# A graph attention layer on one core: the first group's projection goes behind the node table, and a ninth gather slot opens earlier

## The chip, the cores and the metric

The kernel runs on one core of a Trainium2 chip. The metric is the device time of one execution in microseconds (us); lower is better. A core has five engines with their own instruction queues: TensorE (PE in the profile, with its weight loads as PEld), VectorE (DVE), ScalarE (ACT), GpSimd (POOL) and SyncE (SP), which here only issues DMA transfers. Sixteen DMA engines carry all transfers of the core, whichever queue issues them.

## The reference

The input is a graph of 12500 nodes with 128 features each and 212500 edges, sorted by their target node, each with 128 features of its own. The layer computes, per edge, eight attention scores (one for each head of 16 features), and sums the messages at the target:

```python
Q = (x @ WQ).reshape(N, H, dh)
K = (x @ WK).reshape(N, H, dh)
V = (x @ WV).reshape(N, H, dh)
Eh = (edge_attr @ WE).reshape(-1, H, dh)
score = K[src] * Q[dst] / jnp.sqrt(jnp.float32(dh)) * Eh
score = jnp.exp(jnp.clip(score.sum(-1, keepdims=True), -5.0, 5.0))
msg = V[src] * score
wV = jax.ops.segment_sum(msg, dst, num_segments=N)
Z = jax.ops.segment_sum(score, dst, num_segments=N)
h = x + (wV / (Z + ATTN_EPS)).reshape(N, D)
# batch norm of h over the nodes, then layernorm(x + that) per node
```

The costly part is `K[src]` and `V[src]`: a row of 1 KB, from a place that the data chooses, for each of 212500 edges.

## The kernel before

**Tiling.** The edges are cut into 1661 tiles of 128, and the tiles into 208 groups of eight (the last has five). A group is two windows of four tiles; a window's edges point to at most some 64 successive nodes. The work for group g is a chain over the engines: `ehqe` projects the edge features (L560), copies them to `wt` on ACT (L562) and spreads the queries to the edges (L568); `both_halves` multiplies the two on VectorE (L573); `turn_back` transposes the product on PE (L581); `products` multiplies by the keys (L592); `scores` and `clip_exp` make the weights (L598, L606 to L608); `message` weights the values (L616); `onehot` (L521) and `gather_sum` sum the messages by node on PE (L631); `share`, or its steps `denom`, `recip` and `attn`, divides, and `add_x` and `x_out` add the result to `hx`, the transposed features. `q_window`, `q_mm` (L541), `q_hi`, `q_mid` and `q_lo` make a window's queries as three bf16 parts. `turned_onehot` (L531) makes the selection for L568 from target ids that `load_rel` fetches (L401); `load` fetches the edge features (L490).

**The node table.** Before the loop over groups, `table_rows(4 * q)` for q = 0 to 24 computes keys and values of 512 nodes at a time: PE multiplies (L676) into the PSUM banks `ps_e` and `ps_q`, `evac` copies them to a table buffer on ACT and VectorE in turn (L306, L307, L681), and SP stores the buffer to the table `kvd` in memory (L684, the last rows L687). The table buffers are tiles `t` of the pool `tab`, four in rotation, 4 KB per partition each.

**Gathers.** GpSimd gathers rows with one indirect DMA per tile (L225). The first eight groups do not wait for the table: 64 gathers fetch rows of x, and the kernel projects them itself. Groups 0 to 2 are projected among the table's blocks, and groups 3 to 7 in loops 2 to 6 by `project_main` (transposes L322, matmuls L329) into two table buffers each. From group 8 on, the rows come from `kvd` into one of the gather slots (`slot`, 8 KB per partition); these gathers wait for the whole table. In every eighth group or so, from group 18 on, the last tile comes row by row from SP instead (L277).

**Slots.** Eight slots, 0 to 7, exist from the start; four of them first hold the gathered rows of x for groups 0 to 7. `load_kv` takes a free slot and the next pending group and queues its gathers. A slot becomes free when `message(g)` has read it, or when `project_main` has turned the last rows of x in it. Slot 8 is made later: at the end of loop 7 (`FIRST_ROW - 1`) the pool `tab` is closed, a pool `late` is opened in its place, and slot 8, the row buffers `byrow` and the id buffers `rbq` are made in `late`. So group 16 comes into slot 8 and group 17 into the slot that group 8 leaves.

**Order.** The order of each engine's instructions is the order of the program text (`manual_schedule`); semaphores come from the data. In a loop g, `issue()` hands the queued gathers to GpSimd. From g = 8 (`FIRST_ROW`) on, `pace(step)` first makes one of them wait for that loop's `q_mm` on PE as well; whatever is behind it on GpSimd waits with it.

**Early steps.** `steps` lists work for the first groups that is put between the table's blocks, from q = 8 on, one entry per block. Its last entries are `ehqe(0)` and `both_halves(0)` at q = 21, `turn_back(0)`, `q_mm(2)` and `q_hi(2)` at q = 22 and `q_mid(2)` at q = 23. Behind the table come `load_kv()`, `ehqe(1)`, `onehot(0)`, `load(2)`, `turned_onehot(2)`, `load_rel(3)`, `q_window(3)`, `load_rel(4)`, `load(3)`, and then loop 0.

**The end.** When no group is pending, `load_x` puts pieces of x for the last stage into free slots (L477). Slot 8 is left out of that, since its pool closes before the last stage.

Of the kernel before, what the change touches and what calls it, by code (L numbers as in the profile page):

```python
# [8 lines left out]
F32 = mybir.dt.float32  # L9
# [8 lines left out]
P = 128  # L18
# [3 lines left out]
G = 8  # L22
# [3 lines left out]
NSLOT = 8  # L26
# [4 lines left out]
FIRST_ROW = 8  # L31
# [8 lines left out]
def plan(N, T):  # L40

    n, r = divmod(T - sum(LAST), U)
    sizes = [U] * n + [r] * (r > 0) + list(LAST)
    assert n > 1 and len(sizes) % 2 == 0
    starts = [sum(sizes[:g]) for g in range(len(sizes))]
    cuts = list(range(0, N - 64, CH)) + [N - 64, N]
    due = {}
    thr = [0.0] * len(sizes)
    for j, c in enumerate(cuts[1:]):
        need = (c + (64 if c < N - CH else 24)) * T  # L50
        g = next((g for g, t in enumerate(starts) if t * N >= need), None)
        if g is not None:
            due.setdefault(g, []).append(j)
            thr[g] = float(c)
    return sizes, starts, cuts, due, thr
# [27 lines left out]
def gnn_kernel(  # L83
# [23 lines left out]
    usizes, ustarts, cuts, due, _ = plan(N, T)  # L107
# [9 lines left out]
    rows = ctx.enter_context(tc.tile_pool(name="rows", bufs=1))  # L117
# [5 lines left out]
    tab = tps.enter_context(tc.tile_pool(name="table", bufs=1))  # L123
    late = []
# [85 lines left out]
    free = list(range(NSLOT))  # L210
    pending = list(range(nxg, NG))
# [1 line left out]
    steady = [False]  # L213

    def slot(i):
        return (rows if i < NSLOT else late[0]).tile([P, 2 * G * P], F32, name=f"slot{i}")

    def kv_view(g, t):
        SLOT[g] = t[0]
# [9 lines left out]
    queued = []  # L229
# [18 lines left out]
    for (_, n), groups in zip(ROW_STREAMS, row_plan(usizes)):  # L248
# [6 lines left out]
        if tot % n:  # L255
            q = tot // n
# [22 lines left out]
    def load_kv():  # L279
        while free and pending and table[0]:  # L280
            g = pending.pop(0)
            i = free.pop(0)
            kv_view(g, (i, slot(i)))
            for j in range(sizes[g] - (g in by_row)):
                queued.append((gather, KV[g](j, j + 1, 0, 2 * P).rearrange("p a d -> p (a d)"), kvd,
                               starts[g] + j))
            if not steady[0]:
                issue()

    for g in range(nxg):  # L290
        if g % 2 == 0:
            PAIR[g // 2] = free.pop(0)
            t = slot(PAIR[g // 2])
# [198 lines left out]

    def project_main(g):

        half = [tab.tile([P, 4, 2 * P], F32, name="t", bufs=4) for _ in range(2)]
        KV[g] = lambda a, b, c, n=P: half[a // 4][:, a % 4:a % 4 + b - a, c:c + n]
        turn_x(g, 0, True)
        turn_x(g, 4, True)
        yield
        for a in (0, 4):  # L500
            project(g, a, lambda: turned().rearrange("p (a b) d -> p a (b d)", b=2), True)
            yield
# [36 lines left out]
    def q_mm(g):  # L539
        PQ[g] = small_ps[:, 0, :]  # L540
        return nc.tensor.matmul(PQ[g], XW[g], w_q, start=True, stop=True)  # L541

    def q_hi(g):
        Q3[g] = wp.tile([P, 3, P], BF16, name="q3", bufs=2)
        nc.scalar.activation(Q3[g][:, 0, :], PQ[g], AF.Copy, scale=0.25)

    def q_mid(g):
        QR[g] = wp.tile([P, P], F32, name="qr", bufs=1)
        nc.vector.scalar_tensor_tensor(QR[g], PQ[g], 0.25, Q3[g][:, 0, :], op0=OP.mult, op1=OP.subtract)
        nc.scalar.activation(Q3[g][:, 1, :], QR[g], AF.Copy)  # L550
# [4 lines left out]
    def ehqe(g):  # L555

        QE[g], WT[g] = [], []
        for a, b in halves(g):
            eh = psp.tile([P, U * P], F32, name="ps_e", bufs=2)[:, :(b - a) * P]
            nc.tensor.matmul(eh, w_e, EA[g][:, a:b, :].rearrange("p a b -> p (a b)"), start=True, stop=True)  # L560
            t = wp.tile([P, U * P], F32, name="wt", bufs=2)
            nc.scalar.activation(t[:, :(b - a) * P], eh, AF.Copy)  # L562
            WT[g].append(t)
            QE[g].append(psp.tile([P, U * P], F32, name="ps_q", bufs=2)[:, :(b - a) * P])
        for k in range(3):
            for h, (a, b) in enumerate(halves(g)):
                r = slice(h * WN, (h + 1) * WN)
                nc.tensor.matmul(QE[g][h], Q3[g][r, k, :], OT[g][r, :(b - a) * P], start=(k == 0), stop=(k == 2))  # L568
# [6 lines left out]
    def turn_back(g):  # L575

        PW[g] = []
        for h, (a, b) in enumerate(halves(g)):
            ps = turned()
            for j in range(b - a):  # L580
                nc.tensor.transpose(ps[:, j, :], WT[g][h][:, j * P:(j + 1) * P], ident)  # L581
            PW[g].append(ps)
# [84 lines left out]
    NB = -(-N // P)  # L667

    def table_rows(b):
        t = tab.tile([P, 4, 2 * P], F32, name="t", bufs=4)  # L670
        for q in range(b, min(b + 4, NB), 2):
            ps = wide()
            m = min(2, NB - q)
            for i in range(m):
                n = min(P, N - (q + i) * P)
                nc.tensor.matmul(ps[:n, i, :], hx[:, (q + i) * P:(q + i) * P + n], w_kv, start=True, stop=True)  # L676
            fl = min(m, N // P - q)
            if fl:
                step = evac(t[:, q - b:q - b + fl, :], ps[:, :fl, :])
            if fl < m:  # L680
                nc.vector.tensor_copy(t[:n, q - b + fl, :], ps[:n, fl, :])  # L681
        full = min(4, N // P - b)
        if full > 0:
            nc.sync.dma_start(kvd[b * P:(b + full) * P, :].rearrange("(c p) d -> p c d", p=P), t[:, :full, :])  # L684
        if b + 4 > N // P and N % P:
            r0 = N // P * P
            nc.sync.dma_start(kvd[r0:N, :], t[:N - r0, N // P - b, :])  # L687
        while len(queued) > max(0, nxg * G - 11 - 12 * (b // 4 + 1) // 5):
            pace(step)

    NQ = -(-NB // 4)
# [4 lines left out]
    def both_halves(g):  # L696
        both(g, 0)
        both(g, 1)


    steps = [[(locate,)], [(place, runs[0])], [], [(q_mm, 0), (q_hi, 0)],
             [(q_mid, 0), (load_rel, 0)], [(q_lo, 0), (load, 0)], [(q_mm, 1), (q_hi, 1), (load_rel, 1)],
             [(q_mid, 1)], [(q_lo, 1), (load_rel, 2)], [(load, 1)], [(turned_onehot, 0)],
             [(turned_onehot, 1)], [], [(ehqe, 0), (both_halves, 0)], [(turn_back, 0), (q_mm, 2), (q_hi, 2)],
             [(q_mid, 2)]]
    first_step = NQ - len(steps) - 1
    assert first_step > 3 and max(piece) < first_step + 14
    windows = {first_step + 2: (0, 1), first_step + 8: (2,)}
    for q in range(NQ):
# [5 lines left out]
        for g, a in piece.get(q, []):  # L715
            if a == 0:
                i = free.pop(0)
# [11 lines left out]
        f(*a)  # L729
    table[0] = True  # L730
    load_kv()
    ehqe(1)
    onehot(0)
    within(load, 2)
# [48 lines left out]
    for g in range(NG - 2):  # L783
        within(load, g + 4)
        within(load_rel, g + 5)
        if (g + 6) % RQ == 0 and (g + 6) // RQ in quads:
            load_quad((g + 6) // RQ)
        fetch_rows(g)
        within(products, g)
        within(both_halves, g + 1)  # L790
        step = within(add_x, g - 3)
        step = within(q_mm, g + 3) or step
        if step is not None and queued and g >= FIRST_ROW:
            pace(step)
        issue()
        within(gather_sum, g - 1)
        if g + 1 < nxg and g + 1 not in SLOT:
            for _ in project_main(g + 1):
                pass
        within(turn_back, g + 1)  # L800
        within(scores, g)
        within(clip_exp, g)
        within(q_hi, g + 3)
        within(x_out, g - 3)
        within(sums_out, g - 1)
        within(q_lo, g + 2)
        within(denom, g - 2)
        within(recip, g - 2)
        within(attn, g - 2)
        within(q_window, g + 4)  # L810
        within(turned_onehot, g + 3)
        within(ehqe, g + 2)
        within(q_mid, g + 3)
        within(message, g)
        within(onehot, g + 1)
        if g == 2:
            load_last()
        for r in runs[1:]:
            if g == max(4, r[0] // 2 - 12):
                place(r)  # L820
        within_checks(g)
        if NSLOT in free and not pending:
            free.remove(NSLOT)
        while free and todo and not pending:
            load_x()
        bn_parts(2 * g - 5, 2 * g - 3)
        if g == NG - 5:
            assert done >= set(range(NPRE))
            norm_first()
        if g == 4:  # L830
            nc.vector.tensor_scalar(row_ids, row_ids, 8 * P, None, op0=OP.mult)
        if g == FIRST_ROW - 1:
            tps.close()
            late.append(tps.enter_context(tc.tile_pool(name="late", bufs=1)))
            free.append(NSLOT)
            load_kv()
    last = NG - 1
    g = last - 1
# [10 lines left out]
    step = add_x(g - 3)  # L849
# [315 lines left out]
```

## Time and profile before

| what | us |
|---|---|
| median of 3 runs | 2115.63 |
| fastest and slowest of them | 2113.8 and 2118.93 |
| the profiled execution | 2117.82 |
| its span, first to last instruction | 2116.0 |
| mean granted clock of TensorE | 0.928 |

A page of the profile gives busy time by engine, the costliest groups of instructions and the chain that ended last. A row of a group reads: line, engine, operation, what it writes and reads, how many, then its busy time and the mean of one in ns, and behind the second bar the time that the engine stood idle just before these instructions, and what ended most of that. A row of the timeline reads: start in us from the span's start, length in us, engine, line, operation, tiles, shapes, how many were merged into the row; in square brackets stands the idle time of the engine before it and what ended it. Rows of waits read: who waited on whom, total us, times, the longest. Where the releaser is called "issue", the engine waited for nothing that the profile shows. Windows by stretch give each engine's busy time and its number of instructions, then the granted clock of TensorE as a share of full speed, the busy share of the DMA engines and GB/s. Times inside the kernel are us from the start of the span.

### The profile page before, as it was taken

How to read it: one execution, taken by the hardware profiler on the slowest of the kernel's cores; microseconds unless marked ns; L12 is line 12 of the kernel's file. 1: busy time of each engine (PE TensorE's matmuls, PEld its weight loads, DVE VectorE, ACT ScalarE, POOL GpSimd, SP SyncE). 2: the span in 40 equal slices, each digit the busy share in tenths (PEclk: the TensorE clock that was granted, in tenths of full speed). 3: DMA queues.
4: the chain of work that ended last, by engine and by line, in shares of the span. 5: the costliest groups of instructions: out<-in, count | busy, mean ns of one | idle time of the engine just before them, and what ended most of it. 6: DMA issues, size and time to landing. Idle time of an engine off the chain costs nothing. (4 is left out here: it accounts for less than half of the span.)

```text
span 2116.0 us, 37688 instructions
## 1 busy us (share of the span) xinstructions
PE 1694.3 (80%) x9414; PEld 1103.1 (52%) x9414; DVE 1633.9 (77%) x3601; ACT 635.2 (30%) x2480; POOL 1581.2 (75%) x1673
## 2 busy tenths in 40 slices
PE   8899888887777777787877787878787788787877
PEld 6565555555454445455554554455455455454557
DVE  3559989997787787787777777777777778778777
ACT  2343333332232232222222232322222223223225
POOL 7776777777777777777777777777777777777775
PEclk9999999999999998999999999988999998999989
DMA  8856656666566555566565566565566555564674
GB/s 295 289 184 177 187 175 191 188 190 193 158 187 186 167 175 169 157 187 188 167 180 162 159 186 188 168 178 163 165 186 181 176 172 161 168 189 144 184 264 128
DMA packets 177913, 386.83 MB, mean 183 GB/s; under 512 B 38862, under 2 KB 94711, under 8 KB 177687
## 3 DMA queue, kind: packets, MB, share of 16 engines
q0 software_dynamic: 77552, 210.48, 33.9%
q1 hardware_dynamic: 95972, 171.08, 26.5%
q10 hardware_dynamic: 4163, 2.79, 0.4%
q8 instruction: 77, 1.26, 0.2%
q14 instruction: 149, 1.22, 0.2%
HBM read 364.58 MB, written 19.63 MB: 182 GB/s over the span
## 5 line engine op out<-in xcount | busy, mean ns | idle before, releaser
L225 POOL DMA_INDIRECT slot<-kvd,srcs x1573 | 1492.4, 949 | 487.5 <-issue 414.5
L631 PE MATMUL ps_a<-msg,oh 128*128 128x136 f32 (+1 forms) x3322 | 553.1, 308 | 1.7 <-DVE msg L616 1.7
L592 DVE TENSOR_TENSOR p<-slot,ps_t 128x512 f32<-128x512 f32 (+1 forms) x406 | 267.9, 673 | 323.6 <-DMA slot<-kvd,srcs 250.1
L631 PEld LDWEIGHTS ps_a<-msg,oh 128*128 128x128 f32 (+1 forms) x3322 | 447.6, 177 | 86.3 <-issue 61.7
L560 PE MATMUL ps_e<-ea,w_e 128*128 128x512 f32 x832 | 438.8, 654 | 27.7 <-DMA ea<-eaT 26.0
L607 ACT ACTIVATE ps_m<-s 128x64 f32<-128x64 f32 (+1 forms) x209 | 47.5, 227 | 1243.7 <-DVE s L606 931.4
L581 PE MATMUL ps_t<-ident,wt 128*128 128x128 f32 x1661 | 251.2, 293 | 118.0 <-DVE wt L573 116.4
L656 PE MATMUL ps_m<-ident,at 128*128 128x128 f32 x412 | 97.7, 320 | 227.8 <-DVE oh L524 222.9
L581 PEld LDWEIGHTS ps_t<-ident,wt 128*128 128x128 f32 x1661 | 196.3, 148 | 150.5 <-DVE wt L573 143.1
L573 DVE TENSOR_TENSOR wt<-wt,ps_q 128x512 f32<-128x512 f32 x416 | 265.6, 680 | 8.4 <-PE ps_q L568 7.2
L562 ACT ACTIVATE wt<-ps_e 128x512 f32<-128x512 f32 x416 | 233.5, 586 | 65.7 <-PE ps_e L560 61.8
L598 DVE TENSOR_REDUCE s<-p 128x64 f32<-128x1024 f32 (+1 forms) x209 | 251.9, 1205 | 0.1
L616 DVE TENSOR_TENSOR msg<-slot,ps_m 128x1024 f32<-128x1024 f32 (+1 forms) x205 | 242.2, 1182 | 1.4 <-ACT ps_m L607 1.0
L560 PEld LDWEIGHTS ps_e<-ea,w_e 128*128 128x128 f32 x832 | 158.9, 212 | 149.3 <-issue 110.7
L656 PEld LDWEIGHTS ps_m<-ident,at 128*128 128x128 f32 x412 | 63.6, 194 | 319.7 <-ACT q L550 297.1
L568 PE MATMUL ps_q<-ot,q 64*128 64x512 bf16 x1248 | 174.0, 385 | 0.0
L568 PEld LDWEIGHTS <-q 64*128 64x128 bf16 x1248 | 44.5, 95 | 196.7 <-issue 172.6
L521 DVE TENSOR_TENSOR oh<-ps_m,rel_i 128x512 f32<-128x512 f32 x208 | 142.0, 683 | 0.0
L510 ACT ACTIVATE xw<-hx 128x64 f32 x416 | 83.9, 248 | 66.4 <-issue 53.2
L661 ACT ACTIVATE hx<-ps_m 128x64 f32 x412 | 90.4, 219 | 8.0 <-PE ps_m L657 1.2
L647 DVE SCALAR_TENSOR_TENSOR at<-os,keep,rz 128x128 f32<-128x128 f32 x208 | 73.2, 352 | 25.1 <-PE ps_m L656 1.5
L541 PE MATMUL ps_m<-w_q,xw 128*128 128x128 f32 x416 | 86.2, 291 | 1.0 <-ACT xw L510 0.9
(172 smaller groups left out, 1553.7 us busy)
## 6 DMA issues: line engine op xcount, KB each, us to landing
ea<-eaT SPq DMA_DIRECT2D x207, 512.0 KB
byrow<-kvd SPq DMA_DIRECT2D x3072, 1.0 KB
slot<-kvd,srcs POOLq DMA_INDIRECT x1573
rbq<-relT SPq DMA_DIRECT2D x94, 256.0 KB
kvd<-t SPq DMA_DIRECT2D x24, 512.0 KB
slot<-xT SPq DMA_DIRECT2D x24, 256.0 KB
out<-o SPq DMA_DIRECT2D x23, 256.0 KB
hx<-xT SPq DMA_DIRECT2D x11, 512.0 KB
```

What stands on the lines that cost most here:

```text
L225: return nc.gpsimd.indirect_dma_start(out=out, out_offset=None, in_=table, in_offset=bass.IndirectOffsetOnAxis(ap=srcs[:, e:e + 1], axis=0))
L521: nc.vector.tensor_tensor(one, iota_ps[:, None, :].to_broadcast([P, n, P]), r[:, :n, None].to_broadcast([P, n, P]), op=OP.is_equal)
L560: nc.tensor.matmul(eh, w_e, EA[g][:, a:b, :].rearrange("p a b -> p (a b)"), start=True, stop=True)
L562: nc.scalar.activation(t[:, :(b - a) * P], eh, AF.Copy)
L568: nc.tensor.matmul(QE[g][h], Q3[g][r, k, :], OT[g][r, :(b - a) * P], start=(k == 0), stop=(k == 2))
L573: nc.vector.tensor_tensor(t, t, QE[g][h], op=OP.mult)
L581: nc.tensor.transpose(ps[:, j, :], WT[g][h][:, j * P:(j + 1) * P], ident)
L592: nc.vector.tensor_tensor(PR[g][:, c:d, :], KV[g](c, d, 0), PW[g][i][:, c - a:d - a, :], op=OP.mult)
L598: nc.vector.tensor_reduce(SS[g][:, a:b, :], PR[g][:, a:b, :].rearrange("p t (h d) -> p t h d", d=DH), axis=AX.X, op=OP.add)
L616: nc.vector.tensor_tensor(MSG[g][:, a:b, :P].rearrange("p t (h d) -> p t h d", d=DH), KV[g](a, b, P).rearrange("p t (h d) -> p t h d", d=D ...
L631: nc.tensor.matmul(AGG[g][WN if j >= n else 0:], OH[g][j], MSG[g][:, j, :], start=(j == 0), stop=(j == n - 1))
L656: nc.tensor.matmul(ps, AT[g], ident, start=True, stop=False)
```

## The change

Four things are done.

1. `ehqe(0)`, `both_halves(0)`, `turn_back(0)`, `q_mm(2)`, `q_hi(2)` and `q_mid(2)` leave `steps` and stand behind the table's last rows and `load_kv()`. `first_step` stays 8, so the other steps keep their blocks.
2. Slot 8 is made at the start, in the pool of the other slots. Its two halves serve as two of the four table buffers (`table_tile(q)` for q % 4 of 0 and 1); the pool `tab` keeps two. In `project_main`, even groups use the halves of slot 8 and odd groups the two buffers of `tab`, so group 6 is the last in slot 8.
3. Slot 8 is put on the list of free slots at the end of loop 6 instead of loop 7, and it may serve for pieces of x at the end.
4. `pace` begins with loop 12 instead of loop 8.

```diff
     def slot(i):
-        return (rows if i < NSLOT else late[0]).tile([P, 2 * G * P], F32, name=f"slot{i}")
+        return rows.tile([P, 2 * G * P], F32, name=f"slot{i}")
+
+    first = slot(NSLOT).rearrange("p (h c d) -> p h c d", h=2, d=2 * P)
+
+    def table_tile(q):
+        return first[:, q % 4] if q % 4 < 2 else tab.tile([P, 4, 2 * P], F32, name="t", bufs=2)
...
-        half = [tab.tile([P, 4, 2 * P], F32, name="t", bufs=4) for _ in range(2)]
+        half = [table_tile(2 * (g % 2) + a) for a in (0, 1)]
...
-        t = tab.tile([P, 4, 2 * P], F32, name="t", bufs=4)
+        t = table_tile(b // 4)
...
-             [(turned_onehot, 1)], [], [(ehqe, 0), (both_halves, 0)], [(turn_back, 0), (q_mm, 2), (q_hi, 2)],
-             [(q_mid, 2)]]
-    first_step = NQ - len(steps) - 1
+             [(turned_onehot, 1)]]
+    first_step = NQ - len(steps) - 5
...
     table[0] = True
     load_kv()
+    ehqe(0)
+    q_mm(2)
+    q_hi(2)
+    both_halves(0)
+    q_mid(2)
+    turn_back(0)
     ehqe(1)
...
-        if step is not None and queued and g >= FIRST_ROW:
+        if step is not None and queued and g >= FIRST_ROW + 4:
             pace(step)
...
-        if NSLOT in free and not pending:
-            free.remove(NSLOT)
         while free and todo and not pending:
             load_x()
...
         if g == FIRST_ROW - 1:
             tps.close()
             late.append(tps.enter_context(tc.tile_pool(name="late", bufs=1)))
+        if g == FIRST_ROW - 2:
             free.append(NSLOT)
             load_kv()
```

## The prediction

> **What bounds the kernel now.** I read the page's shares first, then the tile `slot` on GpSimd, then the waits, then the timeline of GpSimd, and only then the place of the change. On the page no engine is full:
>
> ```profile
> span 2116.0 us, 37688 instructions
> PE 1694.3 (80%) x9414; PEld 1103.1 (52%) x9414; DVE 1633.9 (77%) x3601; ACT 635.2 (30%) x2480; POOL 1581.2 (75%) x1673
> ```
>
> The instructions on `slot`, and the waits of GpSimd (total, times, longest), say otherwise:
>
> ```profile
> L225 POOL DMA_INDIRECT slot<-x,srcs x64: 940/944/1152, 3.2 to 82.3; - x64
> L225 POOL DMA_INDIRECT slot<-kvd,srcs x1573: 940/946/1276, 86.6 to 2062.2; - x197
> ...
> POOL slot L225 <- issue: 431.9, 1407, 3.4
> ...
> POOL slot L225 <- PE ps_m L541: 15.4, 34, 5.3
> ```
>
> 1573 gathers of the node table run from 86.6 to 2063.1: 1976.5 us. Each holds GpSimd 0.946 us and the next follows 0.30 later, so they come about every 1.25 us. The "idle" of 414 us is that 0.30 again and again. Only two waits are longer, 3.36 (under issue) and 5.34, and the timeline shows them:
>
> ```profile
> 82.31 0.94 POOL L225 DMA_INDIRECT slot<-x,srcs  x1 [0.30 <-DVE t L681]
> 86.61 0.94 POOL L225 DMA_INDIRECT slot<-kvd,srcs  x1 [3.36 <-issue]
> ...
> 156.57 0.95 POOL L225 DMA_INDIRECT slot<-kvd,srcs  x1 [0.30 <-issue]
> ...
> 165.33 0.95 POOL L225 DMA_INDIRECT slot<-kvd,srcs  x1 [0.30 <-issue]
> 171.62 0.94 POOL L225 DMA_INDIRECT slot<-kvd,srcs  x1 [5.34 <-PE ps_m L541]
> ...
> 181.62 0.95 POOL L225 DMA_INDIRECT slot<-kvd,srcs  x1 [0.30 <-PE ps_a L631]
> ```
>
> So the gathers are one unbroken stream with two holes, one where the table ends and one after group 15 (64 gathers from 86.61). The other engines follow the stream at the end: in the waits VectorE stands 250 us for gathers, and the chain that ended last begins with one.
>
> ```profile
> DVE p L592 <- DMA slot<-kvd,srcs: 250.1, 108, 6.6
> 2055.94 2.74 DMA slot<-kvd,srcs
> ```
>
> What shifts the stream shifts the end by as much. The tail from the last gather (2062.2) to 2116.0, 53.8 us, keeps its length. At most the two holes can go: 3.36 - 0.30 + 5.34 - 0.30 = 8.1 us.
>
> **The change: the table's end.** PE, VectorE and SP there:
>
> ```profile
> 72.61 1.88 PE L560 MATMUL ps_e<-ea,w_e 128*128 128x512 f32 x4
> 74.42 0.82 PE L568 MATMUL ps_q<-ot,q 64*128 64x512 bf16 x6
> 75.17 1.13 PE L676 MATMUL ps_e<-w_kv,hx 128*128 128x256 f32 x4
> ...
> 77.06 1.04 PE L581 MATMUL ps_t<-ident,wt 128*128 128x128 f32 x8
> 77.93 0.39 PE L541 MATMUL ps_m<-w_q,xw 128*128 128x128 f32 x2
> 78.15 1.03 PE L676 MATMUL ps_e<-w_kv,hx 128*128 128x256 f32 x4
> 80.75 1.02 PE L560 MATMUL ps_e<-ea,w_e 128*128 128x512 f32 x2
> 81.62 0.42 DVE L681 COPY t<-ps_e 84x256 f32<-84x256 f32 x1 [0.65 <-ACT t L306]
> 82.20 0.69 SPq L687 DMA_DIRECT2D kvd<-t  x1
> ```
>
> PE has no idle time in these rows, so it sets the pace. The moved PE steps are `ehqe(0)` (72.61 to 75.17, 2.56 us) and `turn_back(0)` with `q_mm(2)` (77.06 to 78.15, 1.09). Without them the table's last matmuls end 3.65 earlier, at 77.1, and the last store (L687) goes out at 78.55. Now that store is free 4.1 us after its issue (82.20 to 86.61 - 0.30). Then it is free at 82.65, before the x gathers' turn ends at 82.31 + 0.94 + 0.30 = 83.55. So the table's gathers start at 83.55, 3.06 earlier, with 0.9 us to spare. Beside PE the moved steps take ACT (two copies to `wt`, `q_hi(2)`, half of `q_mid(2)`) and VectorE (two multiplies, the other half of `q_mid(2)`); they issue no DMA. On SP the stores of the last rows and the loads behind them move up.
>
> **The first loops.** The moved work now lies between the table and loop 0:
>
> ```profile
> 82.94 0.38 SPq L490 DMA_DIRECT2D ea<-eaT  x1
> 83.37 2.37 SPq L401 DMA_DIRECT2D rb<-relT  x4
> 84.60 1.28 DVE L573 TENSOR_TENSOR wt<-wt,ps_q 128x512 f32<-128x512 f32 x2
> 89.01 3.78 PE L560 MATMUL ps_e<-ea,w_e 128*128 128x512 f32 x4 [2.42 <-DMA ea<-eaT]
> 89.81 0.36 DVE L531 TENSOR_SCALAR ot<-rb,wiota 128x512 bf16<-128x512 bf16 x1 [2.37 <-DMA rb<-relT]
> 90.28 1.21 DVE L616 TENSOR_TENSOR msg<-slot,ps_m 128x1024 f32<-128x1024 f32 x1
> 94.29 1.29 DVE L573 TENSOR_TENSOR wt<-wt,ps_q 128x512 f32<-128x512 f32 x2 [0.42 <-PE ps_q L568]
> ```
>
> After: PE runs `ehqe(0)` from 77.1 to about 79.85 (its second half waits until L681 empties the bank). VectorE multiplies both halves to 81.1, PE turns them back by 81.75 (it idles some 0.7 in between), then does `ehqe(1)` in 2.7 until 84.45. `both_halves(1)` on VectorE, 84.60 before, then starts near 84.55: the 3.65 us are spent on a chain that nothing covers now, and no more. But the loads of group 2's edges (L490) and group 3's ids (L401) are issued about 3.65 earlier, at 79.3 and 79.7. By their present 6.1 and 6.4 us (to 89.01 and 89.81) they land near 85.4 and 86.1. PE asked for them at 89.01 - 2.42 = 86.6 and VectorE at 89.81 - 2.37 = 87.4, and with `both_halves(1)` unmoved they still do. The waits of 2.37 and 0.42 on VectorE's line go. With about 0.2 lost behind ACT's `q_hi(3)` (my estimate from VectorE's line, which then has no slack there), the main loop runs 2.6 us earlier. I call that shift d = -2.6.
>
> [...] The rows by stretch, whose granted clock (PEclk) is the third number from the end, show it low just behind the 2.42 us wait:
>
> ```profile
> 86.00:90.00 4.00, 1.58 (x5) 0.85 (x6) 1.59 (x4) 0.97 (x5) 2.78 (x3) 0.70 0.97 260
> 90.00:96.00 6.00, 6.00 (x24) 2.71 (x23) 5.55 (x11) 1.39 (x3) 4.48 (x6) 0.63 0.98 334
> ```
>
> [...]
>
> **The second hole.**
>
> ```profile
> 153.45 1.04 PE L322 MATMUL ps_t<-ident,slot 128*128 128x128 f32 x8
> 160.25 1.27 DVE L616 TENSOR_TENSOR msg<-t,ps_m 128x512 f32<-128x512 f32 x2
> 170.96 0.39 PE L541 MATMUL ps_m<-w_q,xw 128*128 128x128 f32 x2
> 175.40 1.21 DVE L616 TENSOR_TENSOR msg<-slot,ps_m 128x1024 f32<-128x1024 f32 x1
> 182.92 1.21 DVE L616 TENSOR_TENSOR msg<-slot,ps_m 128x1024 f32<-128x1024 f32 x1
> ```
>
> Before, group 16's first gather waits for loop 8's `q_mm` (ends 171.35, gather 0.27 later). After, the ninth slot opens behind loop 6 and is unpaced: it needs `message(6)`, which ended at 161.52 and now ends near 158.9. The stream reaches group 16 at 83.55 + (165.33 + 1.25 - 86.61) = 163.52. No wait. Group 15's slot needs group 7's x rows turned (154.49, now 151.9); the stream asks at 156.57 - 3.06 = 153.51. No wait either.
>
> What is late next is group 17. It takes group 8's slot, freed by `message(8)`: 175.40 + 1.21 + 0.27 = 176.88 before, 174.28 with d. The stream would be there at 163.52 + 10.0 = 173.52. So a wait of 0.8 us remains, put down to VectorE. Group 17 started at 181.62, so the gain is 181.62 less the later of 173.52 and 176.88 + d: 4.74 - d = 7.3 us, at most 8.1. Behind it a loop takes 7.5 us (175.40 to 182.92) against 10 us of a group's gathers: group 18, wanted near 184.3, needs `message(9)` at 181.8, and no further hole opens. The table's start may even slip 0.8 us at no cost.
>
> **The small parts.** Taking the pace from loops 8 to 11 moves nothing else: groups 17 to 19 then wait for their slots alone. The four table buffers keep their rotation; project-and-table writes find the same buffer free as before. The later pool shrinks, and its row buffers wait for `message(7)` as before. The ninth slot may now take the last piece of x one loop earlier, a load of 106 KB; its reader is in the last stage. I cost these at 0, at most 0.5 us either way, the issue of one such load on SP.
>
> **Sum.** 2116.0 - 7.3 = 2108.7 of span; with 1.8 us around it 2110.5 against 2117.8 of the profiled execution. That one stands 2.2 above the median of 2115.6, so for the median 2108.3 (-0.35%).
>
> **Rivals.**
> 1. The loop comes no earlier (d = 0). The DMA engines are 0.97 busy from 86 to 90, and the gathers now start among these loads. Then the gain is 4.7, time 2110.9. Against it: the last stores leave earlier too, and 1 us or more is spare. [...]
> 2. The uncovered chain costs more than I work out: PE, ACT and VectorE pass one half to another, and the loop comes 1.7 later. Gain 3.0, time 2112.6. Only at 4.7 later does nothing remain.
> 3. Slower: two table buffers are now halves of one tile. If a copy into the second half must wait until the store from the first has been read, the table stalls at every fourth block. A store needs 4.1 us, the next copy comes about 1.1 after it: 3.0 x 6 = 18 us. The table and the loops come 18 - 3.65 = 14.3 later, and group 17 starts near 176.9 + 14.3 = 191.2: 9.6 us lost, 2125.2. It passes +0.3% from 2.5 us a stall. Against it, the first matmul starts on one piece of `hx` while three later pieces, issued up to 3.5, are still loading:
>
> ```profile
> 1.67 1.85 SPq L155 DMA_DIRECT2D hx<-xT  x4
> 5.00 2.04 PE L676 MATMUL ps_e<-w_kv,hx 128*128 128x256 f32 x4 [5.00 <-DMA hx<-xT]
> ```
>
> So parts of a tile are waited for apart.
>
> **Numbers.** Forecast 0.66, rivals 0.16, 0.10, 0.08. A measurement of this kernel tells about 0.3% (6.3 us) from no change. Of the forecast's share 0.06 falls short of that, so faster 0.60, same 0.32, slower 0.08. The runs scatter from -1.8 to +3.3 us about their median: 2104.5 below the bound of 8.1 (2107.5), and 2114.5 above rival 2.
>
> **What would show it.** Right: the first table gather at 83.5, no 5 us wait near 166, one of about 0.8 near 174 that ends on VectorE's `msg`, no wait for `ea` at 89, `message(0)` near 88 and `message(8)` near 173. Wrong: stalls of VectorE or ACT on `kvd` stores within the table, the table's first gather past 84.5, or a new hole on GpSimd anywhere behind 185.

## The result, and the profile after

The changed kernel takes 2108.94 us (median of 10 executions, 2107.41 to 2111.63). The kernel before, timed beside it, takes 2115.12 (10 executions, 2112.27 to 2118.93). The ratio is 0.9971 with a 95% interval from 0.9962 to 0.9979: about 6 us less, between 4.4 and 8.0. The forecast was 2108.3.

The page of the changed kernel, with the shares of the engines. In the changed kernel the lines that are named here have numbers five higher than before, so that the gather L225 is now L230, `q_mm` is L546 and `message` is L621:

```profile
span 2106.3 us, 37679 instructions
PE 1692.8 (80%) x9414; PEld 1106.6 (53%) x9414; DVE 1633.1 (78%) x3601; ACT 635.8 (30%) x2480; POOL 1579.5 (75%) x1673
```

The engines do the same work as before. What has moved is the stream of gathers. The tile `slot` on GpSimd (how many, shortest, median and longest in ns, first and last start), and GpSimd's waits (total, times, longest):

```profile
L230 POOL DMA_INDIRECT slot<-kvd,srcs x1573: 942/946/1153, 83.8 to 2053.5; - x197
...
POOL slot L230 <- issue: 431.3, 1415, 0.3
...
POOL slot L230 <- PE ps_m L546: 9.1, 30, 0.3
...
POOL slot L230 <- DVE msg L621: 2.9, 8, 0.8
```

The longest wait for PE's `ps_m` has fallen from 5.3 to 0.3 us, and the longest under "issue" from 3.4 to 0.3. Both holes of before are gone as such. The timeline of GpSimd shows what is left of them:

```profile
83.78 0.94 POOL L230 DMA_INDIRECT slot<-kvd,srcs  x1 [0.82 <-DMA rb<-relT]
...
164.03 0.95 POOL L230 DMA_INDIRECT slot<-kvd,srcs  x1 [0.30 <-issue]
...
174.71 0.94 POOL L230 DMA_INDIRECT slot<-kvd,srcs  x1 [0.78 <-DVE msg L621]
```

The first row starts the table's gathers, the second is group 16 and the third group 17. Of the two idle times well above 0.30, one is at the table's end (0.82), one at group 17 (0.78). Group 17 starts at 174.71 instead of 181.62. That is 6.9 us, and from there to the last gather no other gap above 0.36 us is in the stream.

The two profiled spans differ by 9.7 us (2116.0 and 2106.3), more than the medians. The other 2.8 us lie behind group 17: 1.8 in the 1500 or so gathers that follow (181.62 to 2062.2 before, 174.71 to 2053.5 after; 40 of these gathers took over 1.0 us before, 28 after) and 1.0 in the tail (53.8 and 52.8). All that the change touches there is where the last pieces of x are put. The profiled execution of before was 2.7 above its median (2117.82), and that of after 0.8 below (2108.13), so these 2.8 us are probably for the most part the scatter of single executions.

### The profile page after: what moved, and what is told of

It reads as the page before. It is cut to its first block, busy times and chain, and to the rows that moved or that the text cites. A ratio compares the mean times of both kernels' runs of the same rounds, so it can differ in the third digit from the quotient of the medians.

```text
span 2106.3 us, 37679 instructions
## 1 busy us (share of the span) xinstructions
PE 1692.8 (80%) x9414; PEld 1106.6 (53%) x9414; DVE 1633.1 (78%) x3601; ACT 635.8 (30%) x2480; POOL 1579.5 (75%) x1673
## 4 chain that ended last, share of the span: by engine, by line
DVE 23%; POOL 22%; DMA 21%; issue 16%; PE 13%; SPq 2%; ACT 2%; DVEq 1%; ACTq 0%; POOLq 0%
POOL slot L230 22%; DMA slot<-kvd,srcs 15%; DVE wt L578 6%; DVE msg L621 4%; DVE s L603 3%; DMA rbq<-relT 3%; PE ps_a L636 3%; PE ps_e L565 2%; DVE p L597 2%; DVE oh L526 2%; DMA ea<-eaT 2%; SPq L282 1%; PE ps_t L586 1%; DVE ot L536 1%; PE ps_m L661 1%
## 5 line engine op out<-in xcount | busy, mean ns | idle before, releaser
L230 POOL DMA_INDIRECT slot<-kvd,srcs x1573 | 1491.0, 948 | 480.5 <-issue 415.2
L621 DVE TENSOR_TENSOR msg<-slot,ps_m 128x1024 f32<-128x1024 f32 (+2 forms) x209 | 244.7, 1173 | 1.0 <-ACT ps_m L612 0.7
L546 PE MATMUL ps_m<-w_q,xw 128*128 128x128 f32 x416 | 85.9, 290 | 3.2 <-DVE oh L529 2.8
```

The source lines that it names most:

```text
L230: return nc.gpsimd.indirect_dma_start(out=out, out_offset=None, in_=table, in_offset=bass.IndirectOffsetOnAxis(ap=srcs[:, e:e + 1], axis=0))
L621: nc.vector.tensor_tensor(MSG[g][:, a:b, :P].rearrange("p t (h d) -> p t h d", d=DH), KV[g](a, b, P).rearrange("p t (h d) -> p t h d", d=D ...
```

## The experiments

The kernels ran on three chips. The first four ran on one where the kernel before takes 2115.08 us (33 executions). The others ran on two where the same kernel before takes 2742.8 and 2782.26 us. Ratios are always to the kernel before on the same chip. The changed kernel as it stands was timed only beside 2115.12 us, so it is compared with the first four; on the other two chips it was not run.

### The moved steps, taken back

The changed kernel, with the early steps among the table's blocks again:

```diff
-             [(turned_onehot, 1)]]
-    first_step = NQ - len(steps) - 5
+             [(turned_onehot, 1)], [], [(ehqe, 0), (both_halves, 0)], [(turn_back, 0), (q_mm, 2), (q_hi, 2)],
+             [(q_mid, 2)]]
+    first_step = NQ - len(steps) - 1
...
     load_kv()
-    ehqe(0)
-    q_mm(2)
-    q_hi(2)
-    both_halves(0)
-    q_mid(2)
-    turn_back(0)
     ehqe(1)
```

> The changed kernel with its first part undone: ehqe(0), both_halves(0), turn_back(0) and the steps of q(2) stand among the table's blocks again, slot 8 and the pace stay changed. My theory (GpSimd's stream with the rule that group 17 starts at the later of the stream and message(8)): the first table gather is back at about 86.6, the loops are back where they were before (message(8) ends near 176.6), no hole at group 16, group 17 starts near 176.9, and the time is 4.7 us below the kernel before. Rival (the holes count on their own, and the moved steps are worth the 3.1 us of the table's hole): 5.0 below by the second hole, with group 17 at 176.6. Rival (the moved steps are worth nothing): as fast as the changed kernel, 6 to 7 below.

Measured: 2112.3 us (11 executions), ratio 0.9988 (0.9979 to 0.9997). So by the medians 2.8 us of the gain are left without the moved steps, and about 3.4 us go with them (2112.3 less 2108.94). In the profile PE and VectorE wait for the loads of edge features and target ids again:

```profile
84.98 3.78 PE L565 MATMUL ps_e<-ea,w_e 128*128 128x512 f32 x4 [1.76 <-DMA ea<-eaT]
85.72 0.35 DVE L536 TENSOR_SCALAR ot<-rb,wiota 128x512 bf16<-128x512 bf16 x1 [1.74 <-DMA rb<-relT]
```

These waits are the cause that the prediction gave for d: with the steps among the blocks the loads are asked for before they are there. But the same profile warns against reading one execution alone. In it the table was done early though its steps were back: the last store went out at 78.71, the first table gather at 83.66, `message(8)` ended at 172.63 and group 17 went out at 173.88 (expected were 86.6, 176.6 and 176.9 for the last three). So the loops came earlier than in the changed kernel in spite of the waits. This execution took 2107.69 us, the shortest of its eleven. The median is some 2 us above the profile-based expectation, and this profile can't show why. That part stays open.

### The moved steps alone

The kernel before, with the steps moved and nothing else:

```diff
-             [(turned_onehot, 1)], [], [(ehqe, 0), (both_halves, 0)], [(turn_back, 0), (q_mm, 2), (q_hi, 2)],
-             [(q_mid, 2)]]
-    first_step = NQ - len(steps) - 1
+             [(turned_onehot, 1)]]
+    first_step = NQ - len(steps) - 5
...
+    ehqe(0)
+    q_mm(2)
+    q_hi(2)
+    both_halves(0)
+    q_mid(2)
+    turn_back(0)
     ehqe(1)
```

> The kernel before with the first part alone: the steps stand behind the table, slot 8 and the pace as before. My theory: the table's gathers start near 83.8, but group 16 still waits for loop 8's q_mm, which comes 2.2 us earlier with the loops; the hole grows to about 5.9 us, group 17 starts near 179.4, and the time is 2.2 us below the kernel before. Rival (the start counts on its own): 2.8 below with the hole unchanged at 5.3. Rival (the moved steps lengthen the uncovered chain): no gain.

Measured: 2113.14 us (11 executions), ratio 0.9994 (0.9985 to 1.0003), 1.9 us less by the medians, with an interval that reaches zero. The timeline:

```profile
84.76 0.95 POOL L225 DMA_INDIRECT slot<-kvd,srcs  x1 [1.27 <-DMA rb<-relT]
...
169.33 0.39 PE L541 MATMUL ps_m<-w_q,xw 128*128 128x128 f32 x2
169.99 0.95 POOL L225 DMA_INDIRECT slot<-kvd,srcs  x1 [5.18 <-PE ps_m L541]
```

The table's gathers start 1.85 us earlier, and all of it is given back at group 16, which still waits for loop 8's `q_mm`. What remains in the profile is the loop's own shift: that `q_mm` starts at 169.33 instead of 170.96, 1.6 us earlier, and group 17 starts at 180.00 instead of 181.62. A shift of the stream ahead of a hole is worth nothing unless what ends the hole moves with it.

### The pace from loop 8 on, kept

The changed kernel with one number put back:

```diff
-        if step is not None and queued and g >= FIRST_ROW + 4:
+        if step is not None and queued and g >= FIRST_ROW:
```

> The changed kernel with the pace from loop 8 on again. Group 16 is queued in loop 6 and handed over in loop 7, so it is unpaced. My theory: group 17 now waits for loop 9's q_mm (176.30 + 0.39 + 0.27 = 176.96 instead of 174.71), so the hole there grows from 0.8 to 3.0 and the time is 2.2 us above the changed kernel, 4.7 below the kernel before. Rival (the pace is harmless, as group 16 has its slot early): no difference from the changed kernel.

Measured: 2110.93 us (11 executions), ratio 0.9978 (0.9969 to 0.9987), 2.0 above the changed kernel. Now group 17 waits for `q_mm` of loop 9:

```profile
172.94 1.21 DVE L621 TENSOR_TENSOR msg<-slot,ps_m 128x1024 f32<-128x1024 f32 x1
...
176.00 0.39 PE L546 MATMUL ps_m<-w_q,xw 128*128 128x128 f32 x2
176.66 0.95 POOL L230 DMA_INDIRECT slot<-kvd,srcs  x1 [3.02 <-PE ps_m L546]
```

`message(8)`, which frees the slot, ends at 174.15. The gather then waits another 2.2 us for a `q_mm` that it does not need. So taking the pace from these loops is a needed part of the change. By the medians it is worth about 2 us in it, though the intervals of the two ratios overlap.

### The pace taken away alone

The kernel before, with only that number changed the other way:

```diff
-        if step is not None and queued and g >= FIRST_ROW:
+        if step is not None and queued and g >= FIRST_ROW + 4:
```

> The kernel before with the pace from loop 12 on and nothing else. Slot 8 is still made when the table pool closes, so group 16 needs message(7) (169.09) in place of loop 8's q_mm (171.35). My theory: group 16's first gather at about 169.4 instead of 171.6, hole 3.1 instead of 5.3, time 2.2 us below the kernel before. Rival (the pace alone made the hole): no hole, 5 us below.

Measured: 2113.22 us (11 executions), ratio 0.9992 (0.9982 to 1.0001), 1.9 us less by the medians, with an interval that reaches zero.

```profile
86.48 0.94 POOL L225 DMA_INDIRECT slot<-kvd,srcs  x1 [3.24 <-DMA rb<-relT]
...
166.11 1.27 DVE L616 TENSOR_TENSOR msg<-t,ps_m 128x512 f32<-128x512 f32 x2
168.14 0.94 POOL L225 DMA_INDIRECT slot<-kvd,srcs  x1 [1.86 <-ACT q L550]
```

Both holes are still there, the second one shorter. Without the pace, group 16 was expected to wait for `message(7)`, since slot 8 lies in the room of the table buffers, which `message(7)` is the last to read (so by the code). The trace names another releaser, `q_mid` of loop 7 on ACT (L550). `message(7)` ends at 167.38, 0.76 us ahead of the gather, and elsewhere a gather starts 0.27 behind what released it (`q_mm` ends at 171.35 and the gather starts at 171.62 before). So that it is `message(7)` is not shown; what is shown is that with slot 8 in the later pool group 16 still waits for work at the end of loop 7. In the changed kernel, with the slot made at the start, this wait is gone.

### What the first four say together

Places in us from the span's start, each from the one profiled execution; medians of all executions of the kernel. "Behind" is the profiled span less the start of group 17:

| kernel | last store | first table gather | message(8) ends | group 17 starts | behind | median |
|---|---|---|---|---|---|---|
| before | 82.20 | 86.61 | 176.61 | 181.62 | 1934.4 | 2115.1 |
| steps alone | 78.65 | 84.76 | 174.98 | 180.00 | 1936.3 | 2113.1 |
| pace taken away alone | 80.98 | 86.48 | 175.12 | 178.13 | 1932.2 | 2113.2 |
| changed, pace kept | 77.89 | 83.38 | 174.15 | 176.66 | 1933.1 | 2110.9 |
| changed, steps back | 78.71 | 83.66 | 172.63 | 173.88 | 1932.0 | 2112.3 |
| changed | 78.18 | 83.78 | 174.44 | 174.71 | 1931.6 | 2108.9 |

The part behind group 17 differs by at most 4.7 us between these executions and in no order of the changes. To within that, the end follows group 17's start. The profile of the steps alone is of its longest execution (2118.08). The order of the medians is that of group 17's start, but for two rows. The kernel with the steps back is one, since its profile is of its shortest execution. The other is no more than a tie (2113.1 and 2113.2). The sum of the two edits done alone is 3.8 us, and the whole change, with the slot made at the start as its third edit, brings 6.2. The slot was not tried alone, and differences of this size are within the intervals. That each edit alone leaves a wait is what the traces show, not the times.

The table shows one thing more. From the last store to the end of `message(8)` it is 93.9 to 94.4 us in the three kernels with the steps among the blocks and 96.3 in each of the three with the steps behind the table. So the moved work costs the loops some 2 us there, in every profile, and it pays only as far as the table ends earlier by more than that.

### Loads earlier, steps where they were

To move the loads without the moved work, the kernel before got `load(2)` and `load_rel(3)` in the empty entry of the early steps:

```diff
-             [(turned_onehot, 1)], [], [(ehqe, 0), (both_halves, 0)], [(turn_back, 0), (q_mm, 2), (q_hi, 2)],
+             [(turned_onehot, 1)], [(load, 2), (load_rel, 3)], [(ehqe, 0), (both_halves, 0)], [(turn_back, 0), (q_mm, 2), (q_hi, 2)],
...
-    within(load, 2)
     turned_onehot(2)
-    load_rel(3)
     q_window(3)
```

> The kernel before with load(2) and load_rel(3) moved up into the empty entry at block 20 of the table, and nothing else. It asks whether the shift of the loops came from these two loads. My theory: no waits for ea and rb in loop 0, so the loops come 2.2 to 2.6 us earlier, group 16 starts near 169.2 and the time is 2.2 to 2.6 us below the kernel before, with the table's gathers still at 86.6. Rival (the shift came from the moved steps themselves): loops where they were, no gain. Rival (the loads delay the last stores of the table): first table gather up to 1.5 us later, with no effect on the end.

This ran on the chip where the kernel before takes 2742.8 us. Measured: 2733.75 us (10 executions), ratio 0.9981 (0.9961 to 1.0), with an interval that reaches zero. On that chip the gathers of the table start only at 105.22, and the stream has new holes from there on (5.98, 18.80 and 15.38 us for PE's `ps_t` L322 before group 16). The run does not tell how much of d the loads carry, and it was not repeated on the first chip.

### A delay ahead of message(8), and a later one

If `message(8)` is what group 17 waits for, a delay of VectorE ahead of it delays the stream in full, and the same delay in loop 60 should cost less. The multiplies of `products` are done eight times more, in loop 8 or in loop 60 (the same products into the same place):

```diff
         within(products, g)
+        if g == 8:
+            for _ in range(8):
+                for h, (a, b) in enumerate(halves(g)):
+                    nc.vector.tensor_tensor(PR[g][:, a:b, :], KV[g](a, b, 0), PW[g][h][:, :b - a, :], op=OP.mult)
```

```diff
         within(products, g)
+        if g == 60:
+            for _ in range(8):
+                for h, (a, b) in enumerate(halves(g)):
+                    nc.vector.tensor_tensor(PR[g][:, a:b, :], KV[g](a, b, 0), PW[g][h][:, :b - a, :], op=OP.mult)
```

> The changed kernel with the multiply of products(8) done eight times more in loop 8 (the same result each time), some 9.6 us of VectorE. My theory: message(8) ends 9.6 later, the hole ahead of group 17 grows from 0.8 to 10.4, and the whole time grows by 9.6 us. Rival (VectorE is not the bound and has waits to make it up): the time grows by less than 2 us.

> The changed kernel with the same eight extra multiplies in loop 60 instead of loop 8. My theory: GpSimd is several slots ahead of the loops there, no hole opens in the gathers, and the time is that of the changed kernel within its scatter. Rival (the loops, not the gathers, carry the time): 9.6 us more.

Both ran on the chip of 2742.8. Measured: 2760.53 us (4 executions, ratio 1.0075, 1.0055 to 1.0096) with the delay in loop 8, and 2746.41 us (10 executions, ratio 1.0027, 1.0006 to 1.0047) with the delay in loop 60. The rows of `message(8)` and of group 17, with the delay in loop 8:

```profile
261.90 1.21 DVE L621 TENSOR_TENSOR msg<-slot,ps_m 128x1024 f32<-128x1024 f32 x1
263.38 0.95 POOL L230 DMA_INDIRECT slot<-kvd,srcs  x1 [22.71 <-DVE msg L621]
```

and with the delay in loop 60:

```profile
254.90 1.21 DVE L621 TENSOR_TENSOR msg<-slot,ps_m 128x1024 f32<-128x1024 f32 x1
256.38 0.94 POOL L230 DMA_INDIRECT slot<-kvd,srcs  x1 [13.37 <-DVE msg L621]
```

In both, group 17 starts 0.27 us behind the end of `message(8)`, as in the changed kernel on the first chip (173.23 + 1.21 to 174.71). The hole ahead of it is 9.3 us longer with the delay in loop 8. So the releaser is right: this gather hangs on `message(8)`. The times differ by 14.1 us, but the interval of each ratio is some 11 us wide. The pair was run again on the third chip (2782.26):

> The kernel with eight extra multiplies in loop 8 once more, since in the call before the loads of the edge features came so slowly that the loops and not the gathers carried every kernel's time. Where the gathers carry the time, my theory has message(8) end 9.6 us later, the hole ahead of group 17 at 10.4 instead of 0.8, and the time 9.6 us above the changed kernel, that is 3.4 above the kernel before. Rival (VectorE has waits to make it up): under 2 us above the changed kernel.

> The same extra multiplies in loop 60, once more, for the same reason. My theory: no hole in the gathers, time as the changed kernel (6.2 us below the kernel before). Rival (the loops carry the time): 9.6 us more, 3.4 above the kernel before.

Measured: 2795.0 us (8 executions, ratio 1.0054, 1.0035 to 1.0073) with the delay in loop 8, and 2787.53 us (11 executions, ratio 1.002, 1.0002 to 1.0037) in loop 60. The holes are 23.1 and 13.5 us, so 9.6 apart, and the times 7.5 apart. Taken together, a delay of some 9.5 us ahead of `message(8)` costs 7.5 to 14 us at the end on these chips. On them the stream has other holes as well, so this can't say how a delay passes through on the first chip. Nor does it show that the delay in loop 60 costs nothing, since the changed kernel without a delay was not run there.

### Slot 8 opened at the end of loop 7

```diff
-        if g == FIRST_ROW - 2:
+        if g == FIRST_ROW - 1:
             free.append(NSLOT)
             load_kv()
```

> The changed kernel with slot 8 put on the free list at the end of loop 7 instead of loop 6; it is still made at the start and unpaced. GpSimd's waits come from the data alone. My theory: group 16 still needs message(6) only, so the gathers run as in the changed kernel and the time is the same. Rival (the place in the program counts): group 16 starts after loop 7, near 167, a hole of some 3 us, and about 2.5 us more.

It ran on the chip of 2742.8. Measured: 2751.19 us (10 executions), ratio 1.0028 (1.0009 to 1.0047). Group 16, `message(7)` and group 17 in its timeline:

```profile
235.06 0.95 POOL L230 DMA_INDIRECT slot<-kvd,srcs  x1 [0.30 <-issue]
...
249.04 1.28 DVE L621 TENSOR_TENSOR msg<-t,ps_m 128x512 f32<-128x512 f32 x2
...
258.10 0.95 POOL L230 DMA_INDIRECT slot<-kvd,srcs  x1 [13.29 <-DVE msg L621]
```

Group 16 goes out at 235.06, 15 us before `message(7)` ends, though its queueing now stands behind loop 7 in the text. So the place in the text does not hold GpSimd back; only the data does. What the change needed there was the slot in another place than the later pool. Whether opening it a loop earlier brings any time is not shown, since the changed kernel itself was not run on this chip.

### More rows from SP

The stream of gathers is 1573 long because every eighth group or so has one tile fetched row by row from SP. More such tiles should shorten the stream, if SP has room. `ROW_STREAMS` sets how many rows SP fetches in each loop: 16 serve 24 groups, 20 serve 30 and 24 serve 36:

```diff
-ROW_STREAMS = (("SP", 16),)
+ROW_STREAMS = (("SP", 20),)
```

```diff
-ROW_STREAMS = (("SP", 16),)
+ROW_STREAMS = (("SP", 24),)
```

> The changed kernel with 20 instead of 16 rows per loop fetched by SP, so that 30 instead of 24 groups get their last tile from SP and GpSimd issues 1567 gathers instead of 1573. My theory (the stream's length is the count times 1.25): 6 x 1.25 = 7.5 us below the changed kernel, 13.7 below the kernel before. Rival (SP, which took 4.5 to 8.2 us for 16 rows in a loop, becomes late with the edge features): no gain or a loss, with waits for ea on PE.

> The same with 24 rows per loop: 36 groups, 1561 gathers. My theory: 12 x 1.25 = 15 us below the changed kernel, 21 below the kernel before. Rival: SP needs 7 to 12 us per loop for the rows, more than some loops have, and the waits for ea and byrow eat the gain.

They ran on the third chip. Measured: 3067.9 us (5 executions, ratio 1.1033, 1.0986 to 1.108) and 3419.86 us (5 executions, ratio 1.2287, 1.2252 to 1.2323). PE's waits for edge features (total, times, longest), with 20 and with 24:

```profile
PE ps_e L565 <- DMA ea<-eaT: 769.1, 142, 12.6
```

```profile
PE ps_e L565 <- DMA ea<-eaT: 1135.2, 161, 14.6
```

and in the changed kernel on the first chip:

```profile
PE ps_e L565 <- DMA ea<-eaT: 30.7, 15, 4.5
```

The edge features are loaded from the same queue on SP, behind the rows (in the changed kernel SP issues 16 rows from 1200.19 in 8.18 us and the load at 1208.47), and PE waits for them. With 16 rows it waits 396.9 us for them already on the chip of 2742.8 (the kernel that opens slot 8 behind loop 7), and on the third chip, with more rows, longer still; whether 20 would win on the first chip wasn't tried.

## Why the prediction was right, step by step

**The bound.** Right, as far as the runs can tell. Behind group 17 the profiles of the first chip differ by up to 4.7 us in no order of the changes, which is taken for scatter here; to within that, what shifts that group's start shifts the end. On the other two chips the stream was not the bound (last section).

**The table's end.** The last store was forecast at 78.55 and goes out at 78.18:

```profile
75.81 1.03 PE L681 MATMUL ps_e<-w_kv,hx 128*128 128x256 f32 x4
...
77.34 0.42 DVE L686 COPY slot<-ps_e 84x256 f32<-84x256 f32 x1 [0.58 <-ACT slot L311]
...
78.18 0.93 SPq L692 DMA_DIRECT2D kvd<-slot  x1
```

The gathers were forecast at 83.55 with 0.9 us to spare and start at 83.78 (row above). The step that was off is the price of the last store. From its issue to the release of the gather it now takes 5.3 us (78.18 to 83.78 less 0.30), not 4.1. The traces' semaphore records have the last of the store's landing at 85.60 before and at 82.77 after, 3.4 and 4.6 us behind its issue, and the gather starts 1.0 us behind that in both. So the gather waits for this store; the transfer `rb<-relT` that its row names lands only at 85.81. The spare took most of that up, and the rest, 0.2, cost nothing, as group 17 hangs on `message(8)`. The store is 4.0 us earlier instead of 3.65, and part of that may be scatter: the table above has the same end at 82.20, 80.98 and 78.71 with the steps among the blocks.

**The first loops.** The moved chain runs uncovered on PE and VectorE as forecast, with short waits on PE (the 2.61 us of VectorE are for `ehqe(0)`; it has nothing else to do there):

```profile
78.38 1.12 PE L565 MATMUL ps_e<-ea,w_e 128*128 128x512 f32 x2 [0.69 <-ACT wt L567]
79.17 0.38 SPq L495 DMA_DIRECT2D ea<-eaT  x1
79.60 2.37 SPq L406 DMA_DIRECT2D rb<-relT  x4
80.37 1.28 DVE L578 TENSOR_TENSOR wt<-wt,ps_q 128x512 f32<-128x512 f32 x2 [2.61 <-PE ps_q L573]
81.11 1.25 PE L586 MATMUL ps_t<-ident,wt 128*128 128x128 f32 x8 [0.43 <-DVE wt L578]
84.94 1.29 DVE L578 TENSOR_TENSOR wt<-wt,ps_q 128x512 f32<-128x512 f32 x2 [0.45 <-PE ps_q L573]
86.78 1.88 PE L565 MATMUL ps_e<-ea,w_e 128*128 128x512 f32 x4
87.77 0.34 DVE L536 TENSOR_SCALAR ot<-rb,wiota 128x512 bf16<-128x512 bf16 x1
88.49 1.21 DVE L621 TENSOR_TENSOR msg<-slot,ps_m 128x1024 f32<-128x1024 f32 x1
```

`both_halves(1)` comes at 84.94 (forecast near 84.55), the loads are issued at 79.17 and 79.60 (79.3 and 79.7), and neither PE's `ehqe(2)` nor VectorE's `ot` waits for them: their rows carry no bracket. `message(0)` starts at 88.49 instead of 90.28. That is 1.8 us earlier. The shift d was forecast at -2.6; `message(8)` ends at 174.44 instead of 176.61, so it is -2.2. The term that was mis-sized is the chain: from the last store to the end of `message(8)` the forecast has 95.5 us (78.55 to 176.61 - 2.6), and it took 96.3, against 94.4 before. So the moved work costs 1.9 us there instead of 1.1, and half of the missing 0.8 was made up by luck, since the table ended 0.4 earlier than forecast. Rival 2, that this chain costs more than worked out, was right in kind and far too large: it had the loop 4.3 us behind the forecast, and it is 0.4.

**The clock.** The forecast counts nothing for a fall of PE's clock in the new short waits. That was the author's assumption, set beside no measurement. In the profile of before, PE's waits of 0.33 and 0.93 us (up to 82.09 and 84.90) left the clock at 1.00 (76 to 86), and in the changed kernel the new ones did too. The rows by stretch (busy time of PE, PEld, DVE, ACT and POOL, then PEclk, DMA share and GB/s):

```profile
86.00:90.00 4.00, 3.41 (x18) 1.38 (x15) 3.79 (x8) 1.97 (x8) 2.83 (x3) 1.00 1.04 341
90.00:96.00 6.00, 4.97 (x30) 3.66 (x30) 5.60 (x13) 1.16 (x7) 4.73 (x5) 1.00 0.68 227
```

The granted clock is 1.00 in both, where it was 0.70 and 0.63. `ehqe(2)` takes 1.88 us instead of 3.78. PE's waits of 0.43 to 0.69 us (up to 78.38, 81.11 and 85.28) cost no clock here (1.00 from 76 to 96), nor did one of 1.62 us that ended at 91.03. But before, the clock fell within the wait of 2.42 (1.00 from 86.6 to 87.6, 0.50 from 87.6 to 89.0), and with the steps back it was 0.50 from 86 to 90, behind a wait of 1.76.

**Rival 1** (the loads land no earlier) fell: by the traces' semaphore records the edge features issued at 79.17 land at 85.30 and the first ids issued at 79.60 at 85.81, ahead of the rows at 86.78 and 87.77 that use them. That is 6.1 and 6.2 us behind their issue, against 6.0 and 6.1 before. So they lost nothing, beside the gathers, that a wait shows.

**Rival 3** (halves of one tile wait for each other) fell: within the table no copy into a table buffer is seen to wait for a store. The one copy there that waits for a transfer does so at 15.73 for 4.94 us, put down to a load of ids, and the same copy waits 4.50 before. The one wait put down to a store is ACT's for `xw` (6.4 us), and it is as long before.

**The second hole.** Group 16 was forecast at 163.52 without a wait and starts at 164.03 without one. Group 17 was forecast at 174.28 behind a wait of 0.8 that ends on VectorE's `msg`, and starts at 174.71 behind one of 0.78 on it:

```profile
173.23 1.21 DVE L621 TENSOR_TENSOR msg<-slot,ps_m 128x1024 f32<-128x1024 f32 x1
174.71 0.94 POOL L230 DMA_INDIRECT slot<-kvd,srcs  x1 [0.78 <-DVE msg L621]
...
180.89 1.20 DVE L621 TENSOR_TENSOR msg<-slot,ps_m 128x1024 f32<-128x1024 f32 x1
```

Its formula, the later of the stream and `message(8)`, gives 6.9 us with the measured d, and the trace shows 6.9. The forecast had 7.3. `message(9)` ends at 182.1, and no hole opens behind, as said. The median fell by 6.2.

**The small parts.** That the loops 8 to 11 without the pace move nothing else, as the prediction had it, agrees with the stream: no new hole opens. The pace itself is a part of the gain: kept in the changed kernel it costs 2.0 us by the medians, and taken away alone it brings 1.9, not clear of zero. What opening the slot a loop earlier is worth was not measured.

## What to carry to other kernels

When one stream of small instructions bounds a kernel, the waits in it are the only places to gain, and each wait has a next one behind it: work out when the next late thing comes, and take the later of the two, as was done for `message(8)` here. Do all the edits that a hole needs together, for one alone runs into the next wait (by the medians 1.9 and 1.9 us for two edits alone, 6.2 for all three). And judge a gain of a few us by the medians, since single executions of one kernel differ by as much.

## What the hardware showed that was not expected

**The same order of work, another end.** With the early steps among the blocks, the table's last store went out at 82.20, 80.98 and 78.71 in three kernels whose order up to there is the same (the third has two of its table buffers in slot 8). The place where they part is 40 to 64, with the DMA engines 0.95 to 0.97 busy. In the kernel before:

```profile
40.00:64.00 24.00, 20.52 (x94) 17.49 (x93) 8.39 (x15) 7.47 (x18) 18.21 (x20) 0.93 0.95 313
...
60.02 1.84 PE L329 MATMUL ps_q<-w_kv,xt 128*128 128x256 f32 x4 [3.48 <-ACT xt L306]
```

and in the changed kernel with the steps back:

```profile
40.00:64.00 24.00, 21.81 (x110) 18.94 (x109) 10.48 (x19) 8.43 (x19) 18.21 (x20) 1.00 0.97 320
...
58.22 1.13 PE L334 MATMUL ps_q<-w_kv,xt 128*128 128x256 f32 x4 [2.19 <-ACT xt L311]
```

PE waits 3.48 us for ACT in the one and 2.19 in the other, and the granted clock is 0.93 and 1.00. The waits differ by 1.3 us, and a clock of 0.93 over 24 us costs at most 1.7 us (an estimate, 24 times 0.07). What makes ACT late in the one is not settled, nor is it excluded that the two buffers in slot 8 help in the other. The clean pair is the first two kernels, in which nothing differs up to there: their last stores are 1.2 us apart. So part of the 3.65 us that the moved steps give back to the table can't be told from scatter in a single profile.

**The clock can fall within a short wait, and need not.** With 2.42 us without work on PE (before) and 1.76 (steps back) the granted clock was 0.70 and 0.50 from 86 to 90, and `ehqe(2)` took 3.78 us instead of 1.88. But with the steps alone PE was without work for 1.82 us between 86 and 96 (busy for 3.88 of 4 and 4.30 of 6 us) at a clock of 1.00, and in the changed kernel for 1.96 us up to 16.87, and the clock stayed at 1.00 from 10 to 33. So the length of the wait alone does not decide it; what does is not shown.

**Another chip, 30% slower.** The unchanged kernel takes 2115, 2743 and 2782 us on three chips. The mean granted clock is 0.93 on the first and 0.82 on the second, and from 1200 to 2000 the DMA engines move 174 and 135 GB/s (changed kernel, and the one with the delay in loop 8). There the loads of edge features come late: in the kernel that opens slot 8 behind loop 7, PE waits 397 us for them, against 31 in the changed kernel on the first chip, and GpSimd 418 us for PE's `ps_m`, against 9. In that kernel these waits for `ps_m` are up to 22.0 us long (130 in number), against no wait over 0.9 us ahead of a gather of the table in the changed kernel on the first chip. The stream of gathers no longer carries the time. Nor does any run show that the change gains there. The kernels nearest to it are those with the delay in loop 60 (1.0027 and 1.002 of the time before) and the one that opens slot 8 behind loop 7 (1.0028), and all of them are a little slower than the kernel before. Why these chips differ is open; a forecast from a profile of the first holds for the first.
